# The order of SyncE's transfers in a second attention, and the values last in its second visit

## The chip, the core and the metric

The kernel runs on one core of one Trainium2 chip. A core has five engines with a queue each: TensorE (PE, matmuls; its weight loads are shown as PEld), VectorE (DVE), ScalarE (ACT), GpSimd (POOL) and SyncE (SP), which here only issues DMA transfers. Engines run side by side and wait for one another through semaphores; within one queue the order is fixed. The metric is the device time of one execution in microseconds (us), the median of several runs.

## The reference, cut to what matters

Four residual blocks on x of 16 x 256 x 128: attention a, an expert layer, attention b, the same expert layer again. The change is in attention b alone:

```python
Q, K, V = proj(Wq, bq), proj(Wk, bk), proj(Wv, bv)     # 16 heads of 8
rel_idx = jnp.clip(pos[None, :] - pos[:, None], -128, 128) + 128
E = rel_emb[rel_idx]
scores = (einsum('bnqd,bnkd->bnqk', Q, K) + einsum('bnqd,qkd->bnqk', Q, E)) * inv_sqrt_d
attn = softmax(scores, axis=-1)
out = einsum('bnqk,bnkd->bnqd', attn, V)
out = out.transpose(0, 2, 1, 3).reshape(B, S, H)
return out @ Wo.T + bo
```

x is normalised ahead of it, and added to its result. All is float32.

## The kernel before

Attention b (`attention_b`, its loop is in `main`) takes the 16 batches one after the other. A batch has eight units (U; unit 0 to 7 of a batch): each holds 32 queries of all heads against the 256 keys. Per unit, PE makes the scores (L743), one part from keys and queries, one from the strip of relative positions; DVE takes their maxima (b_nm, L753), ACT the exponentials with their sums (b_pr, L758), and DVE transposes the result into b_pT (`turn`, L768), two units behind. The scores have three buffers in PSUM.

All else of a batch is put between its units by `table`: which functions come before the scores of unit 0, 1, 2, 4, 5, 6, 7. Two of them are visits, in which PE does a few pieces in a row, in the order listed:

- unit 0 (`first`): `project_out` of batch b-2 (L819), the gate logits of b-3 (`gate`, L836), the `queries` and keys of b+1 (`ahead_queries`, L590), the first half of the `values` of b-1 (L777).
- unit 4 (`second`): the second half of the `values` of b-1 (L777), `ahead_values` of b+1 (L656), then the transposes of `gate_channels` of b-2 and `ahead_channels` of b+2 (both in L579).

A visit first issues all its pieces' matmuls, then, in the same order, what copies their results out (`all_of`).

The steps that the text follows, for the batch whose number each has:

- `ahead_queries` (b+1): ACT copies the queries to b_qT (L594) and the keys to b_kT. SP then writes b_qT in four transfers to qs in DRAM (L609), builds b_qsel from b_qT in four (L614), b_kS, the keys with their halves swapped, in two (L616), and reads qs back as z, in two (L620).
- `ahead_masks`: POOL makes b_qd from b_qsel (L636) and b_qb from z (L644), which the scores read. The part of b+1 for its units 0 to 3 is made at unit 4 of b, that for units 4 to 7 at unit 0 of b+1.
- `over_sums` (b-1, at unit 1): DVE takes the reciprocal of the sums, b_inv (L791); SP writes it to DRAM, b_rsd (L793), and reads it back as b_rs in four transfers (L799).
- `normalised` (b-1, at unit 5): POOL multiplies the outputs b_oT by b_rs into b_yT (L811), which `project_out` reads at the next unit 0.
- `gate_rows` (b-2, after the first visit): the statistics of x (DVE) and then xn (POOL, L135 to L139), which `gate_channels` transposes at unit 4.
- `ahead_values`: ACT copies v (L662); SP writes it to DRAM, b_vs (L664), and reads it back as b_vz in four (L668); `ahead_spread` (unit 7) copies this on POOL into b_va.
- `ahead_rows` (b+3, unit 6) and `bias` (unit 2) are POOL's other work.

In `main` the queues of PE, DVE, ACT and POOL keep the order in which the code is written (a manual schedule). SP's order is set by the framework's scheduler. In the list of instructions before, SP has for each batch: qs x4, qsel x4, kS x2, z x2, rsd, rs x4, vs, vz x4.

Of the kernel before, what the change touches and what calls it, by code (L numbers as in the profile page):

```python
# [9 lines left out]
F32 = mybir.dt.float32  # L10
# [7 lines left out]
P = 128  # L18
NB, T, C = 16, 256, 128
NH, DH = 16, 8  # L20
NG, NJ = 4, 4
# [12 lines left out]
QB = 8  # L34
NQB = T // QB
# [35 lines left out]
def hybrid_kernel(ctx: ExitStack, tc: tile.TileContext, io):  # L71
    nc = tc.nc
# [3 lines left out]
    dpool = ctx.enter_context(tc.tile_pool(name="dpool", bufs=2, space=DRAM))  # L76
# [441 lines left out]
    def attention_b(outer):  # L518
# [10 lines left out]
        wpool = outer.enter_context(tc.tile_pool(name="b_w", bufs=1))  # L529
# [31 lines left out]
        mask_h, mask_q = const("mask_h"), const("mask_q")  # L561
        NH2, NN = NH // 2, NQB // 2
        rows_of, xnTs, batch, vz, tall = {}, {}, {}, {}, {}

        bo = wpool.tile([P, C], F32, tag="bo", name="b_bo_")

        def output_bias(pt):
            bv = wpool.tile([P, P], F32, tag="bv", name="b_bv_")
            nc.vector.tensor_copy(bv, b_bv.to_broadcast([P, P]))
            nc.tensor.matmul(pt, bv, wb["o"], start=True, stop=True)  # L570
            nc.vector.tensor_tensor(bo, b_bo, pt, ALU.add)

        def ahead_rows(b):
            rows_of[b] = normalise(b)
# [9 lines left out]
        def ahead_channels(b, pt):  # L584
            xnTs[b] = wpool.tile([P, T], F32, tag="xnT", name=f"b_xnT{b}", bufs=2)
            yield from turned(rows_of.pop(b), xnTs[b], pt)

        def ahead_queries(b, pq):
            for i, n in enumerate("qk"):
                nc.tensor.matmul(pq[:, i, :], wb[n], xnTs[b], start=True, stop=True)  # L590
            yield

            qT = wpool.tile([P, 2, QB, NN], F32, tag="qT", name=f"b_qT{b}")
            nc.scalar.activation(  # L594
                qT.rearrange("p r q n -> p n r q"),
                pq[:, 0, :].rearrange("p (n r q) -> p n r q", r=2, q=QB),
                AF.Identity, bias=bqs, scale=SCALE,
            )
            kT = wpool.tile([P, T], F32, tag="kT", name=f"b_kT{b}", bufs=2)
            nc.scalar.activation(kT, pq[:, 1, :], AF.Identity, bias=b_bk, scale=1.0)  # L600


            kS = wpool.tile([P, T], F32, tag="kS", name=f"b_kS{b}", bufs=2)
            qsel = wpool.tile([P, 2, QB, NN], F32, tag="qsel", name=f"b_qsel{b}")
            qs = dpool.tile([2, 2, QB, DH, NH2, NN], F32, tag="qs", name=f"b_qs{b}")
            halves = [slice(0, 64), slice(64, 128)]
            for r in range(2):
                for c in range(2):
                    nc.sync.dma_start(  # L609
                        qs[r, c].rearrange("q d h n -> (d h) q n"), qT[halves[c], r]  # L610
                    )
            for r in range(2):
                for x in range(2):
                    nc.sync.dma_start(qsel[halves[r], x], qT[halves[r ^ x], r])  # L614
            for r in range(2):
                nc.sync.dma_start(kS[halves[r]], kT[halves[1 - r]])  # L616

            z = wpool.tile([P, 2, NH2, NN], F32, tag="z", name=f"b_z{b}")
            for r in range(2):
                nc.sync.dma_start(  # L620
                    z[halves[r]].rearrange("p c h n -> p c (h n)"),
                    qs[r].rearrange("c q d h n -> (q d) c (h n)"),
                )
            batch[b] = ([], [], kT, kS)
            tall[b] = (qsel, z)

        def ahead_masks(b, t):


            qsel, z = tall[b]  # L630
            part = slice(t * NN // 2, (t + 1) * NN // 2)
            full = [P, NN // 2, NH2, QB]
            qd = wpool.tile([P, NN // 2, 2, NH2, QB], F32, tag="qd", name=f"b_qd{b}_{t}", bufs=2)
            qb_ = wpool.tile([P, NN // 2, 2, NH2, QB], F32, tag="qb", name=f"b_qb{b}_{t}", bufs=2)
            for x in range(2):
                nc.gpsimd.tensor_tensor(  # L636
                    qd[:, :, x],
                    qsel[:, x, :, part].rearrange("p q n -> p n q").unsqueeze(2)
                    .to_broadcast(full),
                    mask_h.unsqueeze(1).unsqueeze(3).to_broadcast(full),  # L640
                    ALU.mult,
                )
            for c in range(2):
                nc.gpsimd.tensor_tensor(  # L644
                    qb_[:, :, c],
                    z[:, c, :, part].rearrange("p h n -> p n h").unsqueeze(3)
                    .to_broadcast(full),
                    mask_q.unsqueeze(1).unsqueeze(1).to_broadcast(full),
                    ALU.mult,
                )  # L650
            batch[b][0].append(qd)
            batch[b][1].append(qb_)
# [19 lines left out]
        def ahead_spread(b):  # L672
            z = vz.pop(b).rearrange("p n (c d) -> p n c d", d=DH)
            for j in range(NG):
                rows = slice(32 * j, 32 * j + 32)
                nc.gpsimd.tensor_copy(vas[b % 2][rows, :, :, :, j], z[rows])

        def all_of(*parts):
            parts = list(parts)
            while parts:  # L680
                parts = [g for g in parts if next(g, parts) is None]

        def begin(psum):


            def half_bank(name, width=T):
                return psum.tile([P, width], F32, tag="m", name=name, bufs=2)

            def pieces():
                ahead_rows(0)  # L690
                output_bias(half_bank("b_pbo", C))
                yield
                all_of(ahead_channels(0, half_bank("b_lnT0")))
                ahead_rows(1)
                yield
                all_of(ahead_queries(
                    0, half_bank("b_pqk0", 2 * T).rearrange("p (i t) -> p i t", i=2)
                ))
                ahead_masks(0, 0)
                ahead_masks(0, 1)  # L700
                yield
                all_of(ahead_values(0, half_bank("b_pv0")))
                ahead_spread(0)
                all_of(ahead_channels(1, half_bank("b_lnT1")))
                ahead_rows(2)
                yield

            if not begun:
                begun.append(pieces())
            return begun[0]  # L710
# [7 lines left out]
        def main(st, place, filling):  # L718
# [6 lines left out]
            probs, sums, rs, outs, yTs, own = {}, {}, {}, {}, {}, []  # L725
# [62 lines left out]
            def over_sums(b):  # L788

                inv = small.tile([P, NQB], F32, tag="inv", name=f"b_inv{b}", bufs=2)  # L790
                nc.vector.reciprocal(inv, sums.pop(b))  # L791
                ds = dpool.tile([DH, NG, NJ, QB * NQB], F32, tag="rs", name=f"b_rsd{b}")
                nc.sync.dma_start(  # L793
                    ds.rearrange("d j c (q n) -> (j c q) d n", n=NQB),
                    inv.unsqueeze(1).to_broadcast([P, DH, NQB]),
                )
                rs[b] = pool.tile([P, QB, NQB], F32, tag="rs", name=f"b_rs{b}", bufs=2)
                for c in range(NJ):
                    nc.sync.dma_start(  # L799
                        rs[b][32 * c : 32 * c + 32].rearrange("p q n -> p (q n)"),  # L800
                        ds[:, :, c].rearrange("d j f -> (d j) f"),
                    )
# [47 lines left out]
            def visit(b, *of_banks):  # L850

                parts, tiles = [], {}
                for n, pieces in of_banks:
# [8 lines left out]

            st.enter_context(
                tc.manual_schedule(
                    engines={getattr(mybir.EngineType, e) for e in ("PE", "DVE", "Activation", "Pool")}
                )
            )
            total = NB * NU
# [15 lines left out]
            def second(b):  # L884
                for_batch(ahead_masks, b + 1, 0)
                visit(
                    b,
                    (2, [(values, -1, 0, P, 1), (ahead_values, 1, P, P + T)]),
                    (3, [(gate_channels, -2, 0, T), (ahead_channels, 2, T, 2 * T)]),
                )  # L890

            def for_batch(f, b, *rest):
                if 0 <= b < NB:
                    f(b, *rest)


            table = {
                0: first,
                1: lambda b: for_batch(over_sums, b - 1),
                2: lambda b: for_batch(bias, b - 1),  # L900
                4: second,
                5: lambda b: for_batch(normalised, b - 1),
                6: lambda b: for_batch(ahead_rows, b + 3),
# [5 lines left out]
            for U in range(total + 2 * NU + 1):  # L909
                b, i = divmod(U, NU)  # L910
# [279 lines left out]
```

## Time and profile before

| what | us |
|---|---|
| runs: median (lowest, highest) | 1597.86 (1592.31, 1600.82) |
| the profiled execution, its time | 1593.99 |
| its span in the profile | 1592.2 |
| PE busy in the span | 1549.8 (97%) |
| DVE busy | 800.3 (50%) |
| ACT busy | 840.6 (53%) |
| POOL busy | 404.0 (25%) |

The shares are averages over stages with different limits. From about 774 to 1124 us the second attention runs; in its steady part (920 to 960 us) PE is busy 39.28 of 40 us, DVE 38.21, ACT 32.01 and POOL 34.46. PE's busy time is partly modelled, since its matmuls are pipelined, so a share near one is not yet the peak. A wait is put down to whatever came last; an idle engine that nobody waits for costs nothing. SP is not counted as busy; its lines give the start of a run of issues and the time that issuing took, not the transfer, which lands later.

### The profile page before, as it was taken

What the parts mean: (1) busy time and instruction counts of PE and PEld (TensorE: products, weight loads), DVE (VectorE), ACT (ScalarE), POOL (GpSimd) and SP (SyncE); (2) the same over time, 40 slices, a digit from 0 to 9 for tenths busy, and PEclk for the clock granted to TensorE, in tenths of its full rate; (3) what the DMA queues carried; (4) which work ended last, traced back from release to release, by engine and by line L of the source; (5) the groups of instructions that cost most, each with busy time, mean ns of one, the idle gap of its engine ahead of it and who ended that gap; (6) DMA issues with size and microseconds to landing.
All of it is one profiled execution on the core that took longest, in us unless ns stands there. A gap on an engine that the chain in (4) does not pass through costs nothing. (4 is left out here: it accounts for less than half of the span.)

```text
span 1592.2 us, 31183 instructions
## 1 busy us (share of the span) xinstructions
PE 1549.8 (97%) x12406; PEld 857.7 (54%) x12406; DVE 800.3 (50%) x1602; ACT 840.6 (53%) x2105; POOL 404.0 (25%) x518
## 2 busy tenths in 40 slices
PE   5999999999999999999999999999999999999998
PEld 4666666644444444444566676676544444444443
DVE  6778788623223322222589999998433133221122
ACT  3666666644443343343577788877644434433442
POOL 5123332100001000003278888886200000000000
PEclk9999999999999999999999999999999999999999
DMA  5111111000222211111122222222000323211210
GB/s 191 28 36 34 28 28 28 15 8 0 70 51 75 66 39 37 37 40 33 21 52 49 45 52 54 52 50 42 11 1 0 79 70 100 57 37 45 47 40 7
DMA packets 174385, 69.90 MB, mean 44 GB/s; under 512 B 74776, under 2 KB 173856, under 8 KB 173984
## 3 DMA queue, kind: packets, MB, share of 16 engines
q1 hardware_dynamic: 173664, 67.54, 18.0%
q8 instruction: 98, 1.61, 0.4%
q10 hardware_dynamic: 576, 0.37, 0.1%
q14 instruction: 47, 0.39, 0.1%
HBM read 50.84 MB, written 12.58 MB: 40 GB/s over the span
## 5 line engine op out<-in xcount | busy, mean ns | idle before, releaser
L939 ACT ACTIVATE hT<-ph,head 128x512 f32<-128x512 f32 x512 | 351.5, 688 | 433.8 <-PE ph L937 432.1
L937 PE MATMUL ph<-xn,w 128*128 128x512 f32 x1024 | 471.5, 597 | 1.1 <-ACT hT L939 1.1
L948 PE MATMUL py<-hT,w 128*128 128x512 f32 x1024 | 461.9, 594 | 0.8 <-ACT logits L841 0.5
L948 PEld LDWEIGHTS py<-hT,w 128*128 128x128 f32 x1024 | 192.9, 190 | 234.9 <-issue 228.9
L937 PEld LDWEIGHTS ph<-xn,w 128*128 128x128 f32 x1024 | 188.8, 190 | 212.4 <-issue 207.7
L1043 DVE SCALAR_TENSOR_TENSOR gy<-py,head,gb 128x512 f32<-128x512 f32 x84 | 63.0, 750 | 429.6 <-PE py L948 423.3
L758 ACT ACTIVATE b_pr<-b_s,b_nm 128x256 f32<-128x256 f32 x512 | 235.9, 474 | 67.5 <-DVE b_nm L753 67.3
L339 DVE TENSOR_REDUCE a_nm<-a_s 128x2 f32<-128x512 f32 x256 | 159.0, 684 | 55.4 <-PE a_t L362 52.6
L753 DVE TENSOR_REDUCE b_nm<-b_s 128x4 f32<-128x1024 f32 x128 | 152.6, 1192 | 22.7 <-PE b_s L743 22.5
L743 PE MATMUL b_s<-b_kT,b_qd 64*64 64x256 f32 x1024 | 160.5, 384 | 0.1
L743 PE MATMUL b_s<-b_kS,b_qd 64*64 64x256 f32 x1024 | 157.2, 384 | 0.0
L768 DVE STREAM_TRANSPOSE b_pT<-b_pr 128x1024 f32<-128x1024 f32 x128 | 157.1, 1227 | 0.0
L743 PE MATMUL b_s<-strip,b_qb 64*64 64x256 f32 x2048 | 157.0, 377 | 0.0
L368 ACT ACTIVATE a_pT<-a_t 128x512 f32<-128x512 f32 x256 | 132.2, 602 | 41.3 <-PE a_t L362 41.3
L135 POOL TENSOR_SCALAR ve<-mv 128x2 f32<-128x2 f32 x64 | 14.8, 231 | 451.8 <-DVE mv L132 451.7
L636 POOL TENSOR_TENSOR b_qd<-b_qsel,head 128x512 f32<-128x512 f32 x64 | 83.9, 1333 | 179.3 <-DMA b_qsel<-b_qT 168.6
L334 PE MATMUL a_s<-a_qk 32*128 32x256 f32 x1024 | 128.3, 388 | 0.0
L362 PE MATMUL a_t<-a_qa,a_qk 32*128 32x256 f32 x1024 | 124.2, 388 | 0.8 <-DVE a_qa L354 0.8
L758 ACT ACTIVATION_READ_ACCUMULATOR b_pr<-b_s,b_nm 128x1 f32 x512 | 104.3, 204 | 0.0
L139 POOL TENSOR_SCALAR xn<-x,mv,rstd 128x128 f32<-128x128 f32 x126 | 100.6, 808 | 6.3
L334 PEld LDWEIGHTS a_s<-a_qk 32*128 32x128 f32 x1024 | 91.5, 184 | 14.6 <-issue 9.0
L743 PEld LDWEIGHTS b_s<-strip,b_qb 64*64 64x64 f32 x2048 | 78.4, 133 | 32.6 <-issue 0.5
(168 smaller groups left out, 1487.6 us busy)
## 6 DMA issues: line engine op xcount, KB each, us to landing
gb<-gd SPq DMA_DIRECT2D x128, 256.0 KB
w<-in_w SPq DMA_DIRECT2D x2, 2048.0 KB
a_qks<-a_qkc SPq DMA_DIRECT2D x15, 256.0 KB
a_qk<-a_qks SPq DMA_DIRECT2D x60, 64.0 KB
x<-in_x SPq DMA_DIRECT2D x16, 128.0 KB
b_qs<-b_qT SPq DMA_DIRECT2D x64, 32.0 KB
b_qsel<-b_qT SPq DMA_DIRECT2D x64, 32.0 KB
b_kS<-b_kT SPq DMA_DIRECT2D x32, 64.0 KB
```

The lines of the kernel that those rows point to most:

```text
L139: (last or nc.gpsimd).tensor_scalar(xn[:, t, :], xs[b][:, t, :], mv[:, t, 0:1], rstd[:, t : t + 1], ALU.subtract, ALU.mult,)
L334: nc.tensor.matmul(sc[:, t, :], q[b][rows, g, t * P : (t + 1) * P], k[b][rows, g, :], start=True, stop=True,)
L339: nc.vector.tensor_reduce(nms[G % 4][:, :, j, 0:1].rearrange("p t o -> p (t o)"), sc, AX.X, ALU.max, negate=True,)
L362: nc.tensor.matmul(sc[:, t, :], k[b][rows, g, t * P : (t + 1) * P], qaug[G][rows, :], start=True, stop=True,)
L368: nc.scalar.activation(pT, sc, AF.Exp)
L743: nc.tensor.matmul(sc[64 * c : 64 * c + 64, r, u, :], (qb_[rows, at, c] if rel else qd[rows, at, x]).rearrange("p h q -> p (h q)"), strip[ ...
L753: nc.vector.tensor_reduce(nm, sc, AX.X, ALU.max, negate=True)
L758: nc.scalar.activation(pr[:, u, r, :], sc[:, r, u, :], AF.Exp, bias=nm[:, r, u : u + 1], scale=1.0, accum_out=sums[b][:, n : n + 1],)
L768: nc.vector.transpose(pT[:, half % 2, 4 * i : 4 * i + 4].rearrange("p n k h q -> p (n k h q)"), probs.pop(U).rearrange("p u r k -> p (u r ...
L937: nc.tensor.matmul(ph, w1[:, m * P : (m + 1) * P], xn2[c], start=True, stop=True)
L939: nc.scalar.activation(hT, ph, AF.Gelu_apprx_tanh, bias=b1[:, m : m + 1], scale=1.0)
L948: nc.tensor.matmul(py, w2[:, e * NHC + k, :], hs[k], start=k == 0, stop=k == NHC - 1)
```

## The change

Five things are changed:

- SP joins the engines whose queue keeps the written order in `main`.
- In `ahead_queries` the kS transfers are taken out, into a function of its own, `ahead_keys`; z follows right after qsel. qs has its two leading dimensions swapped, so that z can be read in one transfer for all 128 partitions.
- `over_sums` ends with the write of the reciprocals; reading them back is a function of its own, `sums_back`. At unit 1 the order is `over_sums`, `ahead_keys`, `sums_back`.
- In the second visit the values come last, behind `ahead_values` and the transposes (the first visit has them last already).
- For batch 0, made ahead in `begin`, `ahead_keys(0)` follows the queries.

In the list of instructions after, SP has for each batch: qs x4, qsel x4, z, rsd, kS x2, rs x4, vs, vz x4. On PE the second half of the values has moved behind L656 and L579, and on ACT the copy of b_oT behind the three others of that visit. DVE's order is the same; POOL's differs only in the masks of batch 0.

```diff
-            for r in range(2):
-                for c in range(2):
+            for c in range(2):
+                for r in range(2):
                     nc.sync.dma_start(
-                        qs[r, c].rearrange("q d h n -> (d h) q n"), qT[halves[c], r]
+                        qs[c, r].rearrange("q d h n -> (d h) q n"), qT[halves[c], r]
                     )
             for r in range(2):
                 for x in range(2):
                     nc.sync.dma_start(qsel[halves[r], x], qT[halves[r ^ x], r])
+
+            z = wpool.tile([P, 2, NH2, NN], F32, tag="z", name=f"b_z{b}")
+            nc.sync.dma_start(
+                z.rearrange("p c h n -> p c (h n)"),
+                qs.rearrange("c r q d h n -> (r q d) c (h n)"),
+            )
+            batch[b] = ([], [], kT, kS)
+            tall[b] = (qsel, z)
+
+        def ahead_keys(b):
+
+            kT, kS = batch[b][2:]
             for r in range(2):
                 nc.sync.dma_start(kS[halves[r]], kT[halves[1 - r]])
-
-            z = wpool.tile([P, 2, NH2, NN], F32, tag="z", name=f"b_z{b}")
-            for r in range(2):
-                nc.sync.dma_start(
-                    z[halves[r]].rearrange("p c h n -> p c (h n)"),
-                    qs[r].rearrange("c q d h n -> (q d) c (h n)"),
-                )
-            batch[b] = ([], [], kT, kS)
-            tall[b] = (qsel, z)
...
+                ahead_keys(0)
                 ahead_masks(0, 0)
...
-                ds = dpool.tile([DH, NG, NJ, QB * NQB], F32, tag="rs", name=f"b_rsd{b}")
+                rs[b] = dpool.tile([DH, NG, NJ, QB * NQB], F32, tag="rs", name=f"b_rsd{b}")
                 nc.sync.dma_start(
-                    ds.rearrange("d j c (q n) -> (j c q) d n", n=NQB),
+                    rs[b].rearrange("d j c (q n) -> (j c q) d n", n=NQB),
                     inv.unsqueeze(1).to_broadcast([P, DH, NQB]),
                 )
+
+            def sums_back(b):
+                ds = rs[b]
                 rs[b] = pool.tile([P, QB, NQB], F32, tag="rs", name=f"b_rs{b}", bufs=2)
                 for c in range(NJ):
                     nc.sync.dma_start(
...
-                    engines={getattr(mybir.EngineType, e) for e in ("PE", "DVE", "Activation", "Pool")}
+                    engines={getattr(mybir.EngineType, e) for e in ("PE", "DVE", "Activation", "Pool", "SP")}
...
-                    (2, [(values, -1, 0, P, 1), (ahead_values, 1, P, P + T)]),
+                    (2, [(ahead_values, 1, P, P + T)]),
                     (3, [(gate_channels, -2, 0, T), (ahead_channels, 2, T, 2 * T)]),
+                    (2, [(values, -1, 0, P, 1)]),
...
-                1: lambda b: for_batch(over_sums, b - 1),
+                1: lambda b: (
+                    for_batch(over_sums, b - 1), for_batch(ahead_keys, b + 1),
+                    for_batch(sums_back, b - 1),
+                ),
```

More of the change, by code (lines that the diff above doesn't have):

```diff
@@ L563, in attention_b @@
         rows_of, xnTs, batch, vz, tall = {}, {}, {}, {}, {}
+        halves = [slice(0, 64), slice(64, 128)]
         bo = wpool.tile([P, C], F32, tag="bo", name="b_bo_")
@@ L605, in ahead_queries @@
             qs = dpool.tile([2, 2, QB, DH, NH2, NN], F32, tag="qs", name=f"b_qs{b}")
-            halves = [slice(0, 64), slice(64, 128)]
-            for r in range(2):
-                for c in range(2):
+            for c in range(2):
+                for r in range(2):
                     nc.sync.dma_start(
-                        qs[r, c].rearrange("q d h n -> (d h) q n"), qT[halves[c], r]
+                        qs[c, r].rearrange("q d h n -> (d h) q n"), qT[halves[c], r]
                     )
```

## The prediction

> **What bounds the kernel now.** I read the profiled execution's time first (1593.99 us, of which the span is 1592.2), then the chain of work that ended last. It is TensorE (PE) matmuls of the last expert stage and says nothing of the second attention, so I went to that stage (about 774 to 1124 us) and read the waits there by engine. The columns are: who waited, for whom, us in total, times, longest.
>
> ```profile
> PE b_m L819 <- POOL b_yT L811: 12.3, 12, 2.4
> POOL b_yT L811 <- DMA b_rs<-b_rsd: 25.7, 12, 3.0
> SPq L799 <- DMA b_rsd<-b_inv: 32.2, 15, 3.4
> ```
>
> PE stalls in one place, project_out (L819), for b_yT; GpSimd (POOL) makes b_yT late because it waits for the reciprocal sums b_rs; and SyncE (SP) issues b_rs late. How late is in the timeline of SP's queue (start, length, what):
>
> ```profile
> 887.41 2.66 SPq L609 DMA_DIRECT2D b_qs<-b_qT  x4
> 890.17 3.35 SPq L614 DMA_DIRECT2D b_qsel<-b_qT  x4
> 893.63 1.17 SPq L616 DMA_DIRECT2D b_kS<-b_kT  x2
> 894.90 1.28 SPq L620 DMA_DIRECT2D b_z<-b_qs  x2
> 896.28 0.54 SPq L793 DMA_DIRECT2D b_rsd<-b_inv  x1
> 900.03 1.72 SPq L799 DMA_DIRECT2D b_rs<-b_rsd  x4
> 901.85 0.38 SPq L664 DMA_DIRECT2D b_vs<-b_v  x1
> ```
>
> b_inv is ready at 890.0, but its write waits its turn behind twelve other issues until 896.28. The timelines of POOL and PE give what follows:
>
> ```profile
> 880.61 0.85 POOL L811 TENSOR_TENSOR b_yT<-b_oT,b_rs 128x256 f32<-128x256 f32 x1 [2.22 <-DMA b_rs<-b_rsd]
> 892.97 1.58 POOL L139 TENSOR_SCALAR xn<-x,mv,rstd 128x128 f32<-128x128 f32 x2
> 903.15 0.85 POOL L811 TENSOR_TENSOR b_yT<-b_oT,b_rs 128x256 f32<-128x256 f32 x1 [2.85 <-ACT b_pr L758]
> 881.52 0.71 PE L819 MATMUL b_m<-b_w,b_yT 128*128 128x128 f32 x4 [0.36 <-POOL b_yT L811]
> 892.58 1.95 PE L777 MATMUL b_m<-b_pT,b_va 128*32 128x128 f32 x64
> 894.46 0.71 PE L656 MATMUL b_m<-b_w,b_xnT 128*128 128x128 f32 x4
> 895.01 0.60 PE L579 MATMUL b_m<-head,xn 128*128 128x128 f32 x4
> ```
>
> L819 starts 0.91 us after b_yT does (0.85 of work and the signal). From L819 to L819 is one batch; the eleven steady ones run from 837.19 to 1080.72, a mean of 22.14 us. The table by window (length, PE busy, ..., granted PE clock) shows two of them, and two short stretches:
>
> ```profile
> 881.52:904.04 22.52, 21.31 (x404) 15.25 (x404) 21.21 (x28) 17.51 (x72) 18.85 (x23) 1.00 0.25 49
> 904.04:925.48 21.44, 21.32 (x405) 15.26 (x405) 19.38 (x27) 17.59 (x72) 18.82 (x22) 1.00 0.26 52
> 815.00:820.00 5.00, 5.00 (x76) 3.83 (x79) 2.14 (x3) 3.51 (x14) 4.72 (x7) 0.66 0.17 26
> 1080.00:1085.00 5.00, 4.28 (x40) 3.36 (x44) 2.77 (x3) 3.33 (x15) 3.77 (x6) 0.66 0.17 26
> ```
>
> PE's busy time is the same 21.3 in every steady batch; the rest is the wait at L819. After its two longest stalls there (2.37 us before 814.75, 1.83 before 1080.72) PE got a clock of 0.66 over 5 us, which is 0.34 x 5 = 1.7 us lost each time. A stall of 1.4 (837.19 to 859.88 is 22.69 with 21.30 busy) was followed by a full clock.
>
> **The second limit.** VectorE (DVE) is nearly full. After the short batch its timeline has no gap over 0.1 us between these two:
>
> ```profile
> 920.10 1.23 DVE L753 TENSOR_REDUCE b_nm<-b_s 128x4 f32<-128x1024 f32 x1 [0.83 <-PE b_s L743]
> 931.34 1.22 DVE L753 TENSOR_REDUCE b_nm<-b_s 128x4 f32<-128x1024 f32 x1
> ```
>
> The first follows PE's unit 4, 16.06 after L819 at 904.04; the second is the next batch's unit 0, whose scores PE has 5.8 after its own L819. So a batch can't be shorter than about 16.06 + 11.2 - 5.8 = 21.45, and whatever delays unit 4 adds to it.
>
> **The change part by part.**
> (1) SP's order. In the two instruction lists SP goes from qs x4, qsel x4, kS x2, z x2, rsd, rs x4, vs, vz x4 to qs x4, qsel x4, z x1, rsd, kS x2, rs x4, vs, vz x4. Ahead of rsd this removes two kS issues (1.17 + 0.1 between issues = 1.27) and one z issue (0.62 + 0.05): 1.93. The kS issues now stand where SP waits for rsd's landing: from the end of rsd's issue to rs it waits 1.84 (941.42 to 943.26) up to 3.45 (1006.43 to 1009.88), more than 1.27. Should rsd ever land sooner, 1.27 would come back.
> (2) One z of 128 partitions. Its issue isn't in the trace: by the nearest rows 0.38 (vs, 128 partitions) to 0.62 (each half); I take 0.62. It waits for all four qs landings; rsd, kS, rs, and so b_yT, queue behind it. By the rsd rows a landing takes 1.84 to 3.45 after the issue ends, and qsel with its gaps covers 2.7; so it costs 0 to 0.75. I take 0, the nearer case. D, the gain of the chain to b_yT, is then 1.2 to 2.2; in batches where kS or z took longer (kS up to 2.0 at 1002.36, z up to 2.19 at 1070.51) up to 3.7. I take 2.0, near the plain batches' 1.93. The changed order of the qs loop issues the same four transfers: nothing.
> (3) kS later: the next batch's scores want it some 10 us after; the pair lands by about 15 after L819, well ahead. vs and vz move up with rs; vs needs b_v, copied at 897.64, and would be issued at about 899.9: still covered.
> (4) Values last in the second visit. PE's work is the same, but gate_channels (L579) now comes 1.88 earlier in it, 0.55 after the visit's start: 11.06 + 0.55 = 11.61 after L819, its second transpose at 11.73. It needs xn from POOL, which ends at 894.55, 13.0 after L819: at present 0.46 ahead of its use. That cover goes. ScalarE (ACT) copies b_oT behind three others, 0.8 later (898.3 for 897.50); b_yT, then at about 901, doesn't wait for it. The values' own input, b_pT, gets 1.1 us more room.
>
> **The sum.** b_yT starts on average 22.14 - 0.91 = 21.23 after the L819 before it. With D = 2.0, and the queries' copy b_qT 0.4 later once DVE has less slack (930.84, after the short batch, is 5.36 after its L819; 886.65 and 908.85 are 5.13 and 4.81 after theirs), it starts at 19.6. L819 would want it at 21.45 - 0.91 = 20.5: that wait is gone. POOL runs without a gap from b_yT to the end of xn, 894.55 - 880.61 = 13.95. With a period P the xn is there at 19.6 + 13.95 - P after L819, and PE waits s = 33.55 + 0.06 - 11.73 - P = 21.88 - P. With P = 21.45 + s this gives s = 0.2 and P = 21.65. So the change moves the stall: it removes 0.8 a batch and puts 0.2 in another place. Eleven batches: 11 x 0.49 = 5.4 us. The first stall, 2.37, shrinks by D: 2.0. No stall then reaches 1.8, so both half-clock stretches go: 3.4. The last batch with such a wait, 1080.72 to 1104.30, has 0.86 idle: 0.5 of it. In all 11.3 us, 1593.99 to 1582.7. The median of the runs shown is 3.9 above the profiled one; from 1597.86 it gives 1586.5.
>
> The Trainium skill (TensorE: Matmul & The Clock Gate, "Part 1: The HAM clock gate") says that the clock halves after an idle window of about 3.4 us. By that rule stalls of 1.83 and 2.37 need not have cost a clock, and the sum without the 3.4 us would be about 1590. The rows above show the drop behind just these two stalls, and I go by them.
>
> **The rivals.**
> A: the gain is given back at the gate (no change). If z waits its 0.75, D is 1.2 and s = (22.68 - 21.45) / 2 = 0.6, P = 22.06: the eleven batches give 0.9, the first stall 1.2, the clock 3.4, the last 0.3: 5.8, or 1592. For it: 0.46 of cover against a move of 1.88. Against: qsel's four issues lie between.
> B: slower. The same place, L579 waiting for xn, without relief in SP: at D = 0, s = (23.88 - 21.45) / 2 = 1.2 and P = 22.66, 0.52 more on eleven batches, with the first stall and the clock as before: 1603.6. Gain turns to loss in these batches where P is 22.14, at D = 1.0. Should s reach 1.8, the half clock would add 1.7 to each of some 13 batches, 22 us. For it: every batch pays. Against: three issues do leave the chain, and POOL, busy 18.85 of 22, can follow.
> C: better than forecast. The long kS and z issues vanish too (D = 2.4): P is 21.46, and 11 x 0.68 + 2.3 + 3.4 + 0.5 = 13.7: 1584.
>
> **How the numbers follow.** The forecast (1582 to 1590 with C) has 0.57, A 0.28, B 0.15. The range 1579 to 1601 holds all of the forecast with 3 us of the runs' own spread below it, A, and the mild part of B (1601 and less). A measurement of this kernel can tell about 0.5%, 8 us: faster 0.57 (forecast and C), same 0.31 (A and 0.03 of B), slower 0.12 (B with the clock).
>
> **What would show it.** Right: in the changed kernel's waits L819 for b_yT is down from 12.3 to under 3, SP's rsd starts about 7 us after qs (now 8.9), L579 for xn shows about 0.2 a batch (now 0.2 in all), the mean batch is 21.5 to 21.8, and the clock is 1.00 throughout the stage after its start. Wrong: z starts over 1 us after qsel ends, L579 waits over 0.7 a batch, or PE waits as long as before for scores' banks because DVE has no slack left.

## The result, and the profile after

| | before | changed |
|---|---|---|
| runs: median (lowest, highest), us | 1597.50 (1592.31, 1602.91) | 1608.05 (1602.11, 1610.53) |
| the profiled execution, us | 1593.99 | 1602.83 |
| its span, us | 1592.2 | 1601.0 |
| mean of the eleven steady batches, project_out to project_out, us | 22.14 | 23.06 |

The changed kernel is slower: the ratio is 1.0058, with a 95% interval of 1.0044 to 1.0072 (12 runs of each). The forecast was 1586.5, faster. The profiled execution is one of the three fastest of the twelve: the mean PE clock granted over its span is 0.999, and in the nine that took 1606 to 1610.5 us it is 0.993 to 0.997, so the profile shows less than the whole loss of the median.

The spans differ by 8.8 us. The eleven steady batches give 11 x 0.92 = 10.1, the first one 0.4, and what comes ahead of them and behind them gives back 1.2 and 0.5. So the loss lies in the steady batches. In the changed kernel the lines have moved: project_out is L826, the transposes at the gate L580, scores L747, b_nm L757, the values L781, b_yT L818, the write and the read of the sums L797 and L806, z L617, kS L628; ve and xn are still L135 and L139.

The waits in and around the second attention (770 to 1140 us), after (who waited, for whom, us in total, times, longest):

```profile
PE b_m L580 <- POOL xn L139: 18.3, 26, 1.1
PE b_m L826 <- POOL b_yT L818: 0.7, 1, 0.7
POOL ve L135 <- DVE mv L132: 43.6, 13, 10.2
POOL b_yT L818 <- DMA b_rs<-b_rsd: 13.4, 10, 2.4
DVE b_nm L757 <- PE b_s L747: 41.8, 20, 4.8
SPq L806 <- DMA b_rsd<-b_inv: 14.4, 16, 1.8
```

PE's wait for b_yT is gone, as it should be: 12.3 us before, 0.7 now. In its place PE waits at the transposes of the gate for xn, 18.3 in 13 visits, 1.4 each. The third line has grown: POOL's ve waits 13 times for mv, the statistics from DVE, where before it waited 4 times, 13.2 us in all. In both kernels the longest of these waits (10.2 and 8.6) lies behind the last batches; the other twelve, 33.4 us, are about 2.8 each.

SP did what the change asks of it. Its queue, after (start, length, what):

```profile
911.88 4.16 SPq L609 DMA_DIRECT2D b_qs<-b_qT  x4
916.14 2.49 SPq L614 DMA_DIRECT2D b_qsel<-b_qT  x4
918.81 0.46 SPq L617 DMA_DIRECT2D b_z<-b_qs  x1
919.31 0.47 SPq L797 DMA_DIRECT2D b_rsd<-b_inv  x1
919.88 1.18 SPq L628 DMA_DIRECT2D b_kS<-b_kT  x2
921.77 2.56 SPq L806 DMA_DIRECT2D b_rs<-b_rsd  x4
```

Over the eleven steady batches rsd starts 6.57 after qs (8.93 before), and b_yT starts 19.82 after the project_out ahead of it (21.23 before). But project_out starts 3.24 after b_yT, where it started 0.91 after it: b_yT comes earlier, and nobody needs it yet.

The timelines of POOL, PE and DVE through one visit of the gate and the next b_yT, after:

```profile
882.85 0.23 POOL L135 TENSOR_SCALAR ve<-mv 128x2 f32<-128x2 f32 x1 [1.58 <-DVE mv L132]
893.24 0.22 POOL L135 TENSOR_SCALAR ve<-mv 128x2 f32<-128x2 f32 x1
894.36 1.58 POOL L139 TENSOR_SCALAR xn<-x,mv,rstd 128x128 f32<-128x128 f32 x2
903.10 0.85 POOL L818 TENSOR_TENSOR b_yT<-b_oT,b_rs 128x256 f32<-128x256 f32 x1 [1.63 <-DMA b_rs<-b_rsd]
905.89 0.23 POOL L135 TENSOR_SCALAR ve<-mv 128x2 f32<-128x2 f32 x1 [1.95 <-DVE mv L132]
893.59 0.71 PE L659 MATMUL b_m<-b_w,b_xnT 128*128 128x128 f32 x4
895.22 0.33 PE L580 MATMUL b_m<-head,xn 128*128 128x128 f32 x1 [0.92 <-POOL xn L139]
896.00 0.55 PE L580 MATMUL b_m<-head,xn 128*128 128x128 f32 x3 [0.45 <-POOL xn L139]
896.47 1.96 PE L781 MATMUL b_m<-b_pT,b_va 128*32 128x128 f32 x64
900.38 1.22 DVE L757 TENSOR_REDUCE b_nm<-b_s 128x4 f32<-128x1024 f32 x1 [2.63 <-PE b_s L747]
904.94 0.25 DVE L131 BATCH_NORM_STATS2 stats<-x 128x6 f32<-128x128 f32 x1
905.62 0.18 DVE L132 BATCH_NORM_AGGREGATE mv<-stats 128x2 f32<-128x6 f32 x1
```

b_yT ends at 903.95, but POOL's next instruction, ve of `ahead_rows`, can't start: it needs statistics that DVE makes ahead of unit 6, and these end at 905.80. DVE is late because it stood idle for 2.63 us ahead of unit 4's maxima (0.83 before). Unit 4's scores are late because the values now lie ahead of them, behind the transposes, and these had waited for xn, which POOL makes at the end of the run of work that the previous ve began. The chain is closed. Its measured pieces, from the ve of the batch ahead on: ve (882.85) to the second transposes (896.00) 13.15; to unit 4's b_nm (900.38) 4.38; to the next ve (905.89) 5.51. They add up to 23.04, the length of this batch, as they must between one ve and the next. What makes them a loop is that nothing in it has a gap but the waits for the step before: POOL runs on from ve to the end of xn, PE from the second transposes through the values to unit 4, DVE from unit 4's maxima to mv. The steady batches take 23.04 to 23.08.

Before, the two inputs of this run, a free POOL and the statistics, came close together. The same place in the trace of before, behind the b_yT that starts at 880.61:

```profile
881.44 0.23 POOL L135 TENSOR_SCALAR ve<-mv 128x2 f32<-128x2 f32 x1
881.14 0.18 DVE L132 BATCH_NORM_AGGREGATE mv<-stats 128x2 f32<-128x6 f32 x1
```

mv ends at 881.32, ve starts at 881.44 right behind b_yT: no wait is shown, because the late b_yT hid it. In the ten steady batches of before that have this step, mv ends 0.1 to 1.2 ahead of ve, and only once does ve wait for it, for 0.18.

The table by window (length, PE busy, PEld, DVE, ACT, POOL, granted PE clock, DMA share, GB/s), after:

```profile
882.53:905.59 23.06, 21.70 (x409) 15.31 (x405) 20.25 (x27) 17.50 (x73) 18.84 (x22) 1.00 0.25 50
815.00:820.00 5.00, 5.00 (x121) 3.88 (x124) 4.77 (x9) 4.14 (x17) 4.60 (x7) 1.00 0.19 31
1080.00:1085.00 5.00, 4.55 (x108) 3.58 (x111) 2.36 (x3) 3.74 (x16) 5.00 (x6) 1.00 0.43 97
```

PE is idle for 1.4 of each batch. Its busy time is shown 0.4 longer than before (21.70 for 21.31), most of it in the transposes: 0.33 and 0.55 for the two parts, 0.60 when they ran in one. The two stretches with a clock of 0.66 are gone in this execution, as forecast.

### The profile page after: what moved, and what is told of

It is laid out like the page before. It is cut to its first block, busy times and chain, and to the rows that moved or that the text cites. A ratio compares the mean times of both kernels' runs of the same rounds, so it can differ in the third digit from the quotient of the medians.

```text
span 1601.0 us, 31166 instructions
## 1 busy us (share of the span) xinstructions
PE 1551.0 (97%) x12406; PEld 856.1 (53%) x12406; DVE 799.3 (50%) x1602; ACT 838.7 (52%) x2105; POOL 403.7 (25%) x518
## 5 line engine op out<-in xcount | busy, mean ns | idle before, releaser
L757 DVE TENSOR_REDUCE b_nm<-b_s 128x4 f32<-128x1024 f32 x128 | 152.3, 1190 | 41.9 <-PE b_s L747 41.8
L747 PE MATMUL b_s<-b_kT,b_qd 64*64 64x256 f32 x1024 | 160.3, 383 | 0.1
L747 PE MATMUL b_s<-b_kS,b_qd 64*64 64x256 f32 x1024 | 157.0, 383 | 0.0
L747 PE MATMUL b_s<-strip,b_qb 64*64 64x256 f32 x2048 | 156.8, 376 | 0.0
L135 POOL TENSOR_SCALAR ve<-mv 128x2 f32<-128x2 f32 x64 | 14.7, 229 | 482.9 <-DVE mv L132 482.9
L139 POOL TENSOR_SCALAR xn<-x,mv,rstd 128x128 f32<-128x128 f32 x126 | 100.1, 803 | 6.3
L747 PEld LDWEIGHTS b_s<-strip,b_qb 64*64 64x64 f32 x2048 | 78.4, 133 | 32.5 <-issue 0.4
```

The lines of the kernel that those rows point to most:

```text
L139: (last or nc.gpsimd).tensor_scalar(xn[:, t, :], xs[b][:, t, :], mv[:, t, 0:1], rstd[:, t : t + 1], ALU.subtract, ALU.mult,)
L747: nc.tensor.matmul(sc[64 * c : 64 * c + 64, r, u, :], (qb_[rows, at, c] if rel else qd[rows, at, x]).rearrange("p h q -> p (h q)"), strip[ ...
L757: nc.vector.tensor_reduce(nm, sc, AX.X, ALU.max, negate=True)
```

## The experiments

The theory that they test: the loop DVE statistics, ve, POOL's work up to xn, transposes, values, unit 4, DVE. Each kernel was timed beside the kernel before; its median there was 1595.28 for the first four, 1594.45 for the next four and 1595.81 for the last two. "Period" is the mean of the eleven steady batches of the profiled execution. The median of before was 1597.50 when the changed kernel was timed, some 2 us more, so differences between the changed kernel and an experiment are taken here from what each is above or below the kernel before beside it: the changed kernel is 10.6 above.

| kernel | period | median, us | ratio to before (95%) |
|---|---|---|---|
| e1_sp_only | 21.30 | 1579.50 | 0.9898 (0.9876, 0.9920) |
| e2_values_only | 23.29 | 1608.26 | 1.0080 (1.0051, 1.0108) |
| e3_rows_at_3 | 22.14 | 1592.20 | 0.9972 (0.9955, 0.9990) |
| e4_sp_rows_at_3 | 22.14 | 1591.17 | 0.9971 (0.9958, 0.9984) |
| e5_stats_early | 21.73 | 1586.90 | 0.9948 (0.9928, 0.9969) |
| e6_sp_stats_early | 21.60 | 1583.77 | 0.9927 (0.9907, 0.9948) |
| e7_z_in_two | 21.54 | 1582.99 | 0.9920 (0.9897, 0.9944) |
| e8_keys_before_z | 22.08 | 1589.71 | 0.9964 (0.9947, 0.9980) |
| e9_rows_at_5 | 21.86 | 1589.66 | 0.9962 (0.9945, 0.9979) |
| e10_sp_rows_at_5 | 21.30 | 1579.85 | 0.9897 (0.9876, 0.9917) |

### The two parts, each alone

e1 is the change without the move of the values:

```diff
-                    (2, [(ahead_values, 1, P, P + T)]),
+                    (2, [(values, -1, 0, P, 1), (ahead_values, 1, P, P + T)]),
                     (3, [(gate_channels, -2, 0, T), (ahead_channels, 2, T, 2 * T)]),
-                    (2, [(values, -1, 0, P, 1)]),
```

> The changed kernel with the values first again in the second visit; all of the SP part stays. Theory L (the loss is a loop: the statistics of ahead_rows on DVE, POOL's work up to xn, gate_channels, then the values and unit 4 on PE, and back to DVE; the values' 1.88 us are new in it): the loop is 23.04 - 1.88 = 21.16 a batch, under DVE's own 21.45, so batches of about 21.45, no wait of gate_channels for xn, L826 for b_yT under 3 us in all, and 1583 to 1587 us, 0.7 to 0.9% under the kernel before. Rival S (the SP part itself costs, by its written order, the single z or the keys behind the sums): still slower than before, 1600 or more, with PE waiting for b_yT or for xn. Rival N (the SP part brings nothing): about the time of before, 22.1 a batch.

e2 is the kernel before with that move alone:

```diff
-                    (2, [(values, -1, 0, P, 1), (ahead_values, 1, P, P + T)]),
+                    (2, [(ahead_values, 1, P, P + T)]),
                     (3, [(gate_channels, -2, 0, T), (ahead_channels, 2, T, 2 * T)]),
+                    (2, [(values, -1, 0, P, 1)]),
```

> The kernel before with the values last in the second visit, and nothing of the SP part. Theory L: the same loop, 23.04 a batch, as in the changed kernel, with no wait for b_yT in the steady batches (22.14 is enough for SP's chain), gate_channels waiting some 18 us for xn in all; the first stall for b_yT stays, so 1607 to 1612 us. The prediction's own sum (xn follows b_yT without a gap): 22.66 a batch, 1603 us. Rival S: about the time of before.

The two parts have opposite signs. SP's part alone is the fastest kernel of this study, 1579.5, 15.8 us below the kernel before and so 26.3 below the whole change. Its waits, and one batch in its table by window:

```profile
PE b_m L826 <- POOL b_yT L818: 0.4, 1, 0.4
POOL ve L135 <- DVE mv L132: 34.8, 14, 11.2
```

```profile
920.20:941.50 21.30, 21.30 (x409) 15.29 (x405) 20.28 (x27) 17.57 (x73) 18.93 (x22) 1.00 0.25 50
```

There is no line for the transposes, and PE is busy for the whole batch. POOL's ve waits for the statistics here too (at 899.30, for 0.62), but PE doesn't notice: without the values' 1.88 the loop should be about 23.04 - 1.88 = 21.16 long, just under what PE needs, and the trace of e1 agrees:

```profile
910.87 1.58 POOL L139 TENSOR_SCALAR xn<-x,mv,rstd 128x128 f32<-128x128 f32 x2
912.48 0.60 PE L580 MATMUL b_m<-head,xn 128*128 128x128 f32 x4
```

The second transpose follows 0.11 behind the first, at 912.59, and the second half of xn ends at 912.45. In the changed kernel 0.06 lie between the two (895.94 to 896.00), so here 0.08 is to spare in a batch of 21.25: a loop of 21.17. Both the period and the time are lower than was expected of e1 (about 21.45, 1583 to 1587).

The values' move alone is as slow as the whole change (13.0 above the kernel before). Its waits (line numbers of before):

```profile
PE b_m L579 <- POOL xn L139: 15.5, 26, 1.0
PE b_m L819 <- POOL b_yT L811: 4.5, 6, 2.4
POOL ve L135 <- DVE mv L132: 11.1, 7, 3.0
```

Both waits are in it: PE waits for xn in every batch and for b_yT in some. So the move costs by itself, and SP's gain doesn't reach it. Theory L expected no wait for b_yT in the steady batches and 23.04 each; five of them do wait for it, 2.2 us together, and one, of 24.71, has a stretch of half clock, which the last section shows. The period of 23.29 lies nearer to theory L than to the prediction's own 22.66.

### The whole of ahead_rows earlier

e3 is the whole change, e4 SP's part alone, each with `ahead_rows` ahead of unit 3:

```diff
-                6: lambda b: for_batch(ahead_rows, b + 3),
+                3: lambda b: for_batch(ahead_rows, b + 3),
```

> The whole change, with ahead_rows called before unit 3 in place of unit 6, so that its statistics no longer stand between POOL's b_yT and xn, and on DVE fall where it waits for unit 4. Theory L: the loop is cut, POOL reaches xn of gate_rows about 2.7 us sooner, gate_channels no longer waits, DVE's own limit falls by the 0.83 gap, and a batch is about 21.3 to 21.4 (PE's busy time): 1581 to 1586 us. If values last cost by themselves (PE's order, ACT's copy of b_oT), the time stays above that of before, at 22.5 to 23 a batch. Rival S: above before.

> The SP part and ahead_rows before unit 3, values first as before. Theory L: as values first leave the loop at 21.16 anyway, only DVE's limit changes: 21.3 to 21.4 a batch, 1581 to 1585 us, the same as the whole change with ahead_rows before unit 3 within 2 us. If the values in last place are worth something once the loop is cut, this one is slower than that by more than 2 us.

The wait at the gate went, but both kernels were slower than expected, and equally so: 22.23 in nearly every batch of both. The waits of e3, and two lines of its POOL:

```profile
PE b_m L826 <- POOL b_yT L818: 6.7, 12, 0.8
PE b_s L747 <- ACT b_pr L762: 3.8, 12, 0.4
PE b_m L580 <- POOL xn L139: 0.3, 1, 0.3
```

```profile
917.40 0.23 POOL L135 TENSOR_SCALAR ve<-mv 128x2 f32<-128x2 f32 x1 [2.71 <-DVE mv L132]
924.89 0.85 POOL L818 TENSOR_TENSOR b_yT<-b_oT,b_rs 128x256 f32<-128x256 f32 x1
```

Moving POOL's part with the statistics put another chain on PE's path: POOL waits 2.71 for the statistics at unit 3, its xn, the masks and b_yT come behind that wait without a gap, and PE waits at project_out instead. As a test of the first loop these two runs changed too much at once.

### The link alone

e5 is the whole change, e6 SP's part alone, each with DVE's statistics ahead of unit 3 and POOL's ve, rstd and xn left where they were (not shown: the statistics become a function of their own, and `normalise` takes what it left):

```diff
+            def ahead_statistics(b):
+                early_mv[b] = statistics(b)
...
+                3: lambda b: for_batch(ahead_statistics, b + 3),
```

> The whole change, with only VectorE's half of ahead_rows (the statistics) moved from ahead of unit 6 to ahead of unit 3; GpSimd's half (ve, the mask, xn) stays where it was, ahead of unit 6. Theory (the closed loop statistics on DVE, ve, xn, gate transposes on PE, values with unit 4 behind them, nm(4) on DVE, statistics: 23.04 us): the link from DVE to ve is cut, GpSimd runs from b_yT through xn without a gap, the wait of the transposes at the gate falls from 1.1 us at each of 26 to 0.3 or less, the period from 23.06 to between 21.25 and 21.7, the time to 1578 to 1588. Rival 1 (the values' place at the end of the visit costs its own time, whatever GpSimd does: PE starts unit 4 some 1.9 us later and VectorE has nothing to do meanwhile): the wait at the gate goes but the period stays at 22.5 or above, 1597 or more. Rival 2 (xn is late for a reason on GpSimd itself, its own work from b_yT to xn being longer than what is left): the wait at the gate stays near 1 us, the period near 23, 1605.

> SyncE's part of the change alone (values first in the second visit), with the same early statistics. In SyncE's part alone nothing waited at the gate, and the period was 21.25. Theory (there TensorE's own work sets the period, and the statistics' place is nothing to it): the same time within 3 us, 1577 to 1583, period 21.2 to 21.3. Rival (moving the statistics is a gain by itself, and would have speeded any of these kernels): period 21.0 or less, 1574 or less. Other rival (statistics in the middle of the units delay nm of unit 3 and with it the scores): period 21.6 or more, 1586 or more.

e5 takes 18 us off the whole change by moving four small DVE instructions a batch. Its waits (project_out, the gate and ve have moved by eight lines), and POOL behind one b_yT:

```profile
PE b_m L588 <- POOL xn L147: 3.1, 7, 0.6
PE b_s L755 <- ACT b_pr L770: 3.4, 11, 0.4
POOL ve L143 <- DVE mv L134: 8.3, 1, 8.3
```

```profile
899.23 0.86 POOL L826 TENSOR_TENSOR b_yT<-b_oT,b_rs 128x256 f32<-128x256 f32 x1 [1.68 <-DMA b_rs<-b_rsd]
900.06 0.23 POOL L143 TENSOR_SCALAR ve<-mv 128x2 f32<-128x2 f32 x1
911.56 1.58 POOL L147 TENSOR_SCALAR xn<-x,mv,rstd 128x128 f32<-128x128 f32 x2
```

ve follows b_yT at once, xn follows, and PE's wait at the gate falls from 18.3 to 3.1. The values are still last, so the place of the values costs little where this link is cut: e5 and e6 differ by 3.1 us. ACT's later copy of b_oT is in e5 too, so that isn't the cause either. The period is 21.63 or 21.64 in most batches of both, not the 21.25 of e1 (e5's mean, 21.73, is just above the 21.7 expected). PE waits some 0.3 a batch for the exponentials (b_pr), which it doesn't in e1; the likely reason, not tested further, is that the statistics at unit 3 hold up its maxima. That was the other rival of e6, in which the period of 21.6 came and the time stayed a little below the 1586 named.

### The same link, by one unit

e9 is the whole change, e10 SP's part alone, with `ahead_rows` one unit earlier, behind b_yT, so that POOL's order is as it was:

```diff
-                5: lambda b: for_batch(normalised, b - 1),
-                6: lambda b: for_batch(ahead_rows, b + 3),
+                5: lambda b: (for_batch(normalised, b - 1), for_batch(ahead_rows, b + 3)),
```

> The whole change with ahead_rows one unit earlier, ahead of unit 5 and behind b_yT there, so that GpSimd's order is untouched and only VectorE's statistics come one unit (a maximum and a transpose, about 2.36 us) sooner. The dose test of the loop: its three measured pieces (ve to the second transpose at the gate 13.15, from there to nm of unit 4 4.38, from there to ve 5.51, together 23.04) lose 2.36 in the last, 20.7, less than the 21.25 that TensorE needs. Theory: GpSimd's ve no longer waits for the statistics (they end about 903.5 in a batch in which b_yT ends at 903.95), TensorE's wait at the gate falls from 18.3 us in all to under 4, the period to 21.25 to 21.7, the time to 1579 to 1588. Rival (only the early place at unit 3 helped, by work that it took from the second half of a batch): the period stays at 22.5 or above, 1597 or more.

> SyncE's part alone (values first in the second visit) with ahead_rows at unit 5. Nothing waited for these statistics on the path there, and TensorE's own work set the period at 21.25. Theory: no change against SyncE's part alone, period 21.2 to 21.4, 1577 to 1583. Rival (the statistics ahead of unit 5 hold up its maxima and with them the scores' banks, as those ahead of unit 3 did): period 21.6, 1583 to 1586.

One unit is enough for most of it: 16.7 us below the whole change, at a period of 21.86. e9 missed the upper ends of its expectation narrowly (21.7, and 1588), and its wait at the gate, 5.9 us, was to be under 4. Its steady batches alternate between long ones (22.1 to 22.7) and short ones (21.24 to 21.6). In the long ones it is POOL's own work behind a late b_yT that counts:

```profile
898.39 0.86 POOL L818 TENSOR_TENSOR b_yT<-b_oT,b_rs 128x256 f32<-128x256 f32 x1 [2.13 <-DMA b_rs<-b_rsd]
899.23 0.22 POOL L135 TENSOR_SCALAR ve<-mv 128x2 f32<-128x2 f32 x1
910.75 1.58 POOL L139 TENSOR_SCALAR xn<-x,mv,rstd 128x128 f32<-128x128 f32 x2
```

From b_yT to the end of xn are 912.33 - 898.39 = 13.94 here: the run without a gap that the prediction reckoned with (13.95) is what is left once the statistics are out of the way, and it still ends late for PE in every other batch, by 0.8 in this one (0.35 and 0.45 at the two transposes). e10 was as expected: with the values first, nothing hangs on the statistics' place.

Put together, medians by where the values and the statistics stand:

| | statistics ahead of unit 6 | of unit 5 | of unit 3 |
|---|---|---|---|
| values first | 1579.50 (e1) | 1579.85 (e10) | 1583.77 (e6) |
| values last | 1608.05 (the change) | 1589.66 (e9) | 1586.90 (e5) |

Each against the kernel before beside it, the values' place costs 26.3, 9.8 or 3.1 us, by the place of four DVE instructions that the change doesn't touch. By the spans of the profiled executions it is 22.3, 7.0 and 2.7.

### Where SP's gain is from

e7 is e1 with z in two transfers again, e8 is e1 with the keys ahead of z again:

```diff
-            nc.sync.dma_start(
-                z.rearrange("p c h n -> p c (h n)"),
-                qs.rearrange("c r q d h n -> (r q d) c (h n)"),
-            )
+            for r in range(2):
+                nc.sync.dma_start(
+                    z[halves[r]].rearrange("p c h n -> p c (h n)"),
+                    qs[:, r].rearrange("c q d h n -> (q d) c (h n)"),
+                )
```

> SyncE's part alone, with z's read in two transfers again, so that only the keys' new place behind the sums is left of it. It gives back what the single z saved on SyncE: about 0.4 to 0.6 us by the single z's 0.45 us in the profile after. Theory (the chain of SyncE has slack once b_yT no longer ends last): b_yT 0.5 us later, the wait of project_out for it a few tenths at some batches, the period 21.25 to 21.4, 1579 to 1584. Rival (the chain sets the period at any length): each tenth of b_yT's lateness counts in full, the period 21.7 to 21.8, 1587 to 1591.

```diff
+            for r in range(2):
+                nc.sync.dma_start(kS[halves[r]], kT[halves[1 - r]])
...
         def ahead_keys(b):
...
-            for r in range(2):
-                nc.sync.dma_start(kS[halves[r]], kT[halves[1 - r]])
+            return
```

> SyncE's part alone, with the keys ahead of z again, so that only queries first, z in one transfer and the sums in written order are left. It gives back the two key issues ahead of the sums, about 1.2 us. Theory (the chain has slack of about 0.5 us, beyond which it ends last): the period 21.4 to 21.9, the wait of project_out for b_yT back at 0.3 to 0.6 us in most batches, 1583 to 1591. Rival (the chain has slack of more than 1.2 us and the gain came from z alone): 1578 to 1582. Rival (everything came from the keys' place): as before, 1593 or more.

From the start of qs to that of rsd are 8.93 before, 8.20 in e8, 7.49 in e7 and 6.51 in e1. The wait of project_out in e8 was to be 0.3 to 0.6 a batch:

```profile
PE b_m L828 <- POOL b_yT L820: 11.4, 11, 2.8
```

That is 1.0 each, nearly as before, and the period of 22.08 lies above the range expected, though its time lies within it, in the upper part. In e7 some batches wait for b_yT again, 2.4 us in all; its period of 21.54 is above the 21.4 expected, its time within. So the keys' new place carries most of the gain: with it and two z transfers (e7) 11.5 of e1's 15.8 us are there, with the single z and without it (e8) 4.7. The written order of SP's queue is in both, and no run has it alone.

## Why the prediction was wrong

**The step that failed** is "POOL runs without a gap from b_yT to the end of xn, 894.55 - 880.61 = 13.95". It took a run without a gap in the trace of before for a chain, and let xn follow b_yT wherever b_yT went. But ve, the first instruction behind b_yT, depends on DVE's statistics too, which in before end only 0.1 to 1.2 ahead of it. b_yT came 1.4 us earlier in its batch (19.82, forecast 19.6), and the gap opened behind it: b_yT to the end of xn is 15.5 in the batch shown of the changed kernel (880.41 to 895.94) and 16.6 on average over the ten steady ones with this step, 2.6 more than the run without a gap. e5 moves only the statistics of that link, e9 the whole of `ahead_rows` but with POOL's order kept, and they give back 18 and 17 us; in e9's long batches the 13.95 is there again.

**What is late next.** The prediction let the values' move cost 0.2 a batch at the gate, because the stall would be fed by an earlier b_yT. It measured 1.4. It also held xn's lateness and the statistics apart: the values behind the gate delay unit 4, unit 4 delays DVE, and DVE delays the next xn. So the move costs its full length, 1.88 in a loop of 21.17, and the period is 23.04 or more in both kernels that have it with the statistics at unit 6, with SP's gain (the change) and without it (e2).

**SP's chain** (part 1 and 2) was right. D was taken as 2.0; rsd comes 2.35 earlier behind qs. The single z was taken at an issue of 0.62 and took 0.45, with no extra wait: in the batch shown it starts 0.2 after qsel ends. The kS issues did hide behind rsd's landing. The first stall at project_out went from 2.37 to 0.7 (forecast 2.0 less). The queries' copy came 0.5 later (5.55 after project_out, 5.01 before), forecast 0.4.

**The clock** was right for the profiled execution: no 0.66 stretch in the stage after its start. In nine of the twelve executions the clock over the whole span was lower (0.993 to 0.997), and where it fell in them is not shown. That a stall of 1.8 or more costs a clock, on which the sum's 3.4 us rest, doesn't hold by itself: in e8 stalls of 1.86 and 2.81 cost none. The wait for b_yT is gone, as forecast.

**VectorE's floor** of 21.45 was 0.2 too high. Its three terms, taken around one batch, add up to that batch's own length (21.44 for the one from 904.04, in which DVE is busy 19.38), and so can't show a least one. In e1 the same three are 915.03 - 898.98 = 16.05, 926.13 - 915.03 = 11.10 and 926.13 - 920.23 = 5.90, which give 21.25, and there it is PE that is full (21.30 of 21.30) and DVE that has room (20.28).

**The rivals.** Rival B named the right place, L579 waiting for xn, and gave it its price at D = 0: 22.66 a batch, 1603.6, 5.7 above the kernel before. e2, which is that case, took 23.29 and 1608.26, 13.0 above. B shared the failed step: it too let xn hang on b_yT alone, so that an earlier b_yT seemed its cure. The point it named, D = 1.0, at which the loss turns to a gain, was not there: at D = 2.35 the kernel was nearly as slow against before (1.0058) as at 0 (1.0080).

The condition set down for a wrong forecast, "L579 waits over 0.7 a batch", is what came.

## What to carry to other kernels

Two operations that stand back to back without a shown wait need not be one chain: before letting the second follow the first to an earlier time, look up when each of its other inputs is ready, for an input that comes a tenth of a microsecond earlier shows no wait in the profile. Then follow a moved piece of work round the whole loop until it meets itself one iteration later; here work that joined a loop with 0.08 to spare cost nearly its full length in every iteration, whatever slack the chain through SP had gained. A change of two parts is better run as two: here one was worth 1.0%, and the other cost 0.8% alone and 1.6% on top of the first.

## What the hardware showed unexpectedly

The granted clock fell after short stalls, and not by the length of the stall alone. In the kernel before and in e2 and e8 a lower clock, some 1.7 us lost each time, followed single stalls of 2.37 and 1.83, 2.38, and 2.19 us. But in e8 stalls of 1.86 and 2.81 were followed by a full clock; the longer one, and the window behind it:

```profile
948.65 0.71 PE L828 MATMUL b_m<-b_w,b_yT 128*128 128x128 f32 x4 [2.81 <-POOL b_yT L820]
948.65:952.06 3.41, 3.40 (x66) 3.02 (x69) 1.87 (x2) 2.42 (x11) 3.17 (x6) 1.00 0.25 41
```

In e2 a half clock also followed two stalls of 0.96 and 0.44 with 0.33 of work between them; the table by window of e2 shows the stretch:

```profile
1014.60:1018.01 3.41, 3.41 (x64) 2.88 (x60) 0.90 (x1) 2.12 (x10) 3.02 (x3) 0.50 0.47 97
```

The changed kernel has such a pair at the same place in each of its steady batches, most of 0.92 to 0.94 and 0.45 and one of 0.96 and 0.44, and lost no clock there in its profiled execution. What else decides wasn't tried.

One read of z for 128 partitions takes SP 0.45 us to issue in the changed kernel (0.52 in most batches of e8, with the keys ahead of it), and the two of 64 partitions before take 1.28 together in most batches, with the gap between them, and up to 2.19.
